# Masks and adjacency earlier in the first group, and the next norm tied behind the attention's last product

## The chip, the cores and the metric

The kernel runs on one core of a Trainium2 chip. The metric is device time in microseconds (us) of one execution; the median of four runs before the change is 2364.11 us (2363.8 to 2365.03). Engine names are those of the profile: PE is TensorE (PEld its weight load), DVE is VectorE, ACT is ScalarE, POOL is GpSimd, SP is SyncE, which here only issues transfers. Each engine works through its own list of instructions strictly in order; an instruction that waits holds up everything behind it on that engine.

## The reference

A graph attention layer with a norm ahead of it, over 128 graphs of 64 nodes with 512 features, all float32. One adjacency matrix (64 x 64) serves all graphs. Cut to what matters here:

```
h = relu(layernorm(x))                                   # x: [128, 64, 512]
def gat(x, W, a):                                        # W: [H, F, O]
    Wh = einsum('bnf,hfo->bhno', x, W)
    f1, f2 = Wh . a[:, :O], Wh . a[:, O:]
    e = leaky(f1[..., :, None] + f2[..., None, :], 0.01)
    e = where(adj > 0, e, -1e9)
    return einsum('bhnm,bhmo->bhno', softmax(e), Wh)
h   = elu(gat(h, W_heads, a_heads))                      # 4 heads, joined to [b, n, 2048]
out = elu(gat(h, W_out, a_out))                          # 1 head
y   = relu(out @ w1 + b1) @ w2 + b2 + out
x + layernorm(y) * gamma + beta
```

## The kernel before, in words

Two graphs make a tile of 128 rows, so there are 64 tiles; four tiles make a group, and there are 16 groups. The large products (`project1`, `project2`, the two of `feed_forward`) use a seven-product scheme for 2 x 2 blocks (Strassen-Winograd), so sums of blocks are formed ahead of the products on POOL and DVE (`z_sums`, `sums`, the subtractions of `project2`'s `post`).

**A group's way.** `norm1(t)` takes a tile of x through `norm_stats` (L340-350): `bn_stats` (L343), `bn_aggr` (L345) and an add (L347) on DVE, a power (L349) on POOL; then a product on POOL (L357, tile `n1nb`) and the relu with scale and bias on ACT (L359), which writes `hn`. For the last two tiles of a group POOL adds two halves (L362, `hns`). `transpose_h` (L368-373) turns `hn` on PE (`pth`) and copies it to `hT` on ACT. `project_f` makes the scores' terms, `scores1` and `softmax` the attention weights, `transpose_weights` turns them. `attend1` (L510-539) multiplies the weights with `hn` on PE (L525, tiles `pz`, `pzS`); of each pair of result banks ACT copies one (L535) and DVE the other (L537) into `z`. `project1` makes the heads from z, `project2` (L604-628) the second layer's projection; `stage_e` is the second attention and `feed_forward` the rest.

**Who runs beside whom.** The main loop is over groups g. While `project2(g)` runs on PE, `attend1(g + 1)` and the norms, transposes, scores and softmax of group g + 2 are put between its products by `run` (L251-258). So beside `project2(0)` lie `attend1(1)` (tiles 4 to 7) and the norms of tiles 8 to 11.

**What sets the order.** The code's order is not the order on the engines. A scheduler sorts each engine's instructions by dependencies and priorities when the kernel is built, and an instruction may be placed far ahead of where the code has it. Tiles come from pools: `x` has four buffers (L94), `hn` four (L358), so the norm's relu of tile 8 waits until the attention's products of tile 4 have read `hn`, and the load of tile 12 (L95, from `prefetch`) waits until that relu has read x of tile 8. The results of `pth` use a pool of two PSUM buffers (`aux`, L81), those of `pz` and of the projections a pool of six banks (`bank`, L78).

**The queues.** SP issues the loads of x (L95), of the small first inputs (L100, L104, L107) and of all weight pieces (L238), in order. ACT's queue issues the four loads of W_heads (L150) at the start, POOL's the other weights and the stores of their sums (L222).

**The first group.** Before the main loop stand the loads, `norm1` of tiles 0 to 3, `masks()` (L117-135: `wa`, `blkones`, the sums over the identity `id32`, `headrow`, `isf`, `par`, `isq`, the adjacency mask `negm` from `aj`, and `eye`), and `fold_dve` (L173-181: 24 products with a sum on DVE, tile `jk`), which reads the PSUM banks that `spread_a` filled (`pab`, L158). `fold_pe` (L183-197: `pwt`, `wT`, `pwa`) needs banks that `fold_dve` frees.

In code, what the change touches is the order of the first loads and of two calls, and the first instruction of the norm:

```python
    for m in range(H):
        fetch(m)
    for t in range(G):
        norm1(t)
    masks()
    ...
        nc.vector.bn_stats(st, src)
```

Of the kernel before, what the change touches and what calls it, by code (L numbers as in the profile page):

```python
# [22 lines left out]
def gat_preln_kernel(  # L23
# [28 lines left out]
    nc = tc.nc  # L52
    P = 128
    B, N, F = x.shape
# [4 lines left out]
    NB = P // N  # L59
# [32 lines left out]
    def load(t, name="x"):  # L92

        tl = wk.tile([P, F], FP, tag="x", name=f"{name}{t}", bufs=4)  # L94
        nc.sync.dma_start(out=tl, in_=xf[ts(t, P), :])  # L95
        return tl

    X[0] = load(0)
    ar = wk.tile([2 * H, O], FP, tag="elu", name="ar", bufs=3)
    nc.sync.dma_start(out=ar, in_=a_heads.rearrange("h (r p) -> (h r) p", p=O))  # L100
    for t in range(1, G):
        X[t] = load(t)
    ah = wk.tile([2 * H * KC, P], FP, tag="elu", name="ah", bufs=3)
    nc.sync.dma_start(out=ah, in_=a_heads.rearrange("h (r p) -> (h r) p", p=P))  # L104
    aj = const.tile([P, N], mybir.dt.int32, name="aj")
    for b in range(NB):
        nc.sync.dma_start(out=aj[ts(b, N), :], in_=adj)  # L107

    negm = const.tile([P, N], FP, name="negm")
    blkones = const.tile([P, NB, N], FP, name="blkones")  # L110
# [6 lines left out]
    def masks():  # L117

        nc.vector.memset(wa, 0.0)
        id32 = const.tile([P, 32], FP, name="id32")  # L120
        nc.vector.tensor_reduce(id32, ident.rearrange("p (j r) -> p r j", r=32), AX.X, ALU.add)
        nc.vector.tensor_add(headrow, id32[:, 0:H], id32[:, H:2 * H])
        nc.vector.tensor_reduce(isf, id32[:, 0:2 * H].rearrange("p (c h) -> p c h", c=2), AX.X, ALU.add)
        for q in range(2):
            par = sm.tile([P, 1], FP, tag="par", name=f"par{q}")
            nc.vector.tensor_reduce(
                par, ident.rearrange("p (a q r) -> p q a r", a=2, q=2)[:, q], AX.XY, ALU.add
            )
            nc.vector.tensor_scalar(isq[:, q], isf, par, None, ALU.mult)
        nc.vector.memset(blkones, 0.0)  # L130
        for b in range(NB):
            nc.vector.memset(blkones[ts(b, N), b, :], 1.0)
        nc.vector.tensor_scalar(negm, aj, 0.0, None, ALU.is_gt)
        nc.vector.tensor_scalar(negm, negm, NEG, -NEG, ALU.mult, ALU.add)
        nc.vector.tensor_add(eye, ident[:, 0:N], ident[:, N:2 * N])
# [11 lines left out]
    def fetch(m):  # L147
        MT[m] = big.tile([P, KC, O], FP, tag=homes[m], name=f"pw{m}")
        queue = nc.scalar if m < H else nc.gpsimd
        queue.dma_start(out=MT[m], in_=mats[m].rearrange("(k p) o -> p k o", p=P))  # L150
# [88 lines left out]
        return w  # L239


    late = []

    def nothing():
        pass
# [5 lines left out]
    def run(steps, side=()):  # L251

        side, done = list(side), 0
        for i, fn in enumerate(steps):
            fn()
            while done * len(steps) < (i + 1) * len(side):
                side[done]()
                done += 1
# [81 lines left out]
    def norm_stats(src, tag, t):  # L340

        st = sm.tile([P, 6], FP, tag=tag + "st", name=f"{tag}st{t}")
        nc.vector.bn_stats(st, src)  # L343
        mv = sm.tile([P, 2], FP, tag=tag + "mv", name=f"{tag}mv{t}")
        nc.vector.bn_aggr(mv, st)  # L345
        ve = sm.tile([P, 1], FP, tag=tag + "ve", name=f"{tag}ve{t}")
        nc.vector.tensor_scalar(ve, mv[:, 1:2], EPS, None, ALU.add)  # L347
        rstd = sm.tile([P, 1], FP, tag=tag + "rs", name=f"{tag}rs{t}")
        nc.gpsimd.tensor_tensor(rstd, ve, mhalf, ALU.pow)  # L349
        return mv[:, 0:1], rstd  # L350
# [159 lines left out]
    def attend1(g):  # L510
        z = {}
        ZB[g] = z

        def task(j, half):
            t = G * g + j
            nm = ("11", "12")[half] if j < 2 else ("S1", "22")[half]
            if nm not in z:
                z[nm] = big.tile([P, H, 2, T], FP, tag="z" + nm, name=f"z{nm}_{g}")
            src, off = (HNS[t], 0) if nm == "S1" else (HN[t], half * T)
            at = AT[t]  # L520
            banks = [bank(f"pz{nm}_{t}_{b}") for b in range(NB)]
            for c in range(2):
                for b in range(NB):
                    rows = slice(b * N, (b + 1) * N)
                    nc.tensor.matmul(  # L525
                        banks[b][:, c, :].rearrange("p (h n) -> p h n", h=H),
                        src[rows, off + c * P:off + (c + 1) * P],
                        at[rows, b], start=True, stop=True, skip_group_check=True,
                    )
            for b in range(NB):  # L530
                n0 = (j % 2) * P + b * N
                dst = z[nm][:, :, :, n0:n0 + N].rearrange("p h c n -> p c h n")
                srcv = banks[b].rearrange("p c (h n) -> p c h n", h=H)
                if b == 0:
                    nc.scalar.copy(dst, srcv)  # L535
                else:
                    nc.vector.tensor_copy(dst, srcv)  # L537

        return [lambda j=j, half=half: task(j, half) for j in range(G) for half in range(2)]
# [64 lines left out]
    def project2(g):  # L604
        slot = {1: "11", 2: "12", 3: "12", 4: "22", 5: "S1", 6: "11", 7: "S1"}
        h1 = dict(H1)
        wh = big.tile([P, G, FO], FP, tag="wh2", name=f"wh2_{g}")
        WH2[g] = wh

        def post(what, a, b=None, to=None):  # L610
            behind = {"s1": ("11", "S1", "11"), "s5": ("S1", "22", "11"), "c11": ("12", "12", "11")}
            if what in behind:
                dst, x0, x1 = (h1[n] for n in behind[what])
                for h in range(H):
                    nc.gpsimd.tensor_tensor(dst[:, h], x0[:, h], x1[:, h], ALU.subtract)  # L615
            if what[0] != "c":
                return
            r, c = quadrant(what)
            dst = wh[:, 2 * r:2 * r + 2, c * Q:(c + 1) * Q]
            if b is None:  # L620
                nc.scalar.copy(dst, a)  # L621
            else:
                nc.vector.tensor_tensor(dst, a, b, ALU.add)

        ms = [H + h for h in range(H)]
        return unit(
            f"b{g}", product_n(ms, lambda p, i: h1[slot[p]][:, i]), post, (1, 5, 6, 2, 7, 3, 4)
        )
# [136 lines left out]

    for m in range(H):
        fetch(m)
    for t in range(G):
        norm1(t)
    masks()  # L770
    ab = {m: spread_a(m) for m in (0, 1)}
    aT = turn_a()
    for t in range(G):
# [43 lines left out]
    for g in range(NG):  # L817
        if g >= 1:
            side = stage_e(g - 1)
        else:  # L820
            side = sum(stage_a(1), [])
            for i, m in ((5, 4), (9, 5), (12, 6), (17, 7)):
                side.insert(i, lambda m=m: more_sums(m))
        done, n = 0, 6 * H
        for i in range(n):
            if i % 6 == 0:
                steps = head0 if (g, i) == (0, 0) else project1(g, i // 6)
            if (g, i // 2) != (0, 0):
                steps[i % 6]()
            while done * n < (i + 1) * len(side):  # L830
                side[done]()
                done += 1
        flush_late()
        attn = attend1(g + 1) if g + 1 < NG else []
        norms, scores, turns = stage_a(g + 2)
        tr, ff, fin = feed_forward(g - 1) if g >= 1 else ([], [], [])
        if g == NG - 1:
            run(project2(g), tr + [nothing] * 6 + ff[:2])
            run(ff[2:], [
                lambda: [scores2(g, j) for j in range(G)], lambda: spread2(g), nothing, nothing,  # L840
                lambda: softmax2(g), *[nothing] * 7, lambda: transpose_weights2(g), nothing,
                *[lambda j=j: attend2(g, j) for j in range(G)], nothing,
            ])
            continue
        early = [lambda: z_sums(g + 1, 0)]
        first = mix(attn, tr)
        if g >= 1:
            first[5:5] = norms[:1]
            first[10:10] = norms[1:]
        if g == 0:  # L850
            def sums_late(m):
                fetch(m)
                weight_sums(m, LAST["A"])

            run(project2(g), first + early + norms + scores + turns + [
                load_rows, lambda: sums_late(M1), lambda: sums_late(M2)
            ])
        else:
            run(project2(g), first + mix(
                ff[:7] + early + ff[7:12] + fin[:1] + ff[12:13] + fin[1:2] + ff[13:],  # L860
                scores + [nothing] * 8,
            ) + mix(fin[2:], [nothing] + turns + [nothing] * 2))
# [32 lines left out]
```

## Time and profile before

| what | us |
|---|---|
| median of four runs | 2364.11 |
| the profiled execution's own time | 2363.88 |
| its span (first to last instruction) | 2362.1 |
| around the span | 1.8 |
| PE busy | 2319.2 (98%) |
| DVE, ACT, POOL busy | 1264.5, 911.9, 1026.7 |
| PE busy in 0 to 25, 25 to 50, 50 to 118 | 13.73, 17.17, 65.47 |
| PE busy in 118 to 150, 150 to 175 | 26.59, 23.23 |
| PE busy in 175 to 700 | 525.00 |

The last three rows come from the busy time by stretch. From 175 us on PE is busy without a break in the stretches looked at; what PE stands idle lies before that. A line of the timeline reads: start, duration, engine, line, operation, output and input tile, shape, count, and in brackets the idle time before it and what ended that. SPq, ACTq and POOLq lines are transfers being issued. A chain can be followed through the brackets: an instruction's releaser is the one whose end it waited for.

### The profile page before, as it was taken

The numbers are of one execution on the slowest core, as the hardware profiler recorded it, in microseconds if no ns is written. First come the engines' busy times: TensorE is split into PE (matmuls) and PEld (weight loads), VectorE is DVE, ScalarE is ACT, GpSimd is POOL, SyncE is SP. The second block draws the span as 40 slices with busy tenths as digits, with TensorE's granted clock in tenths as the row PEclk, the third lists the DMA queues.
The fourth block names the chain that finished last, engine by engine and source line by source line (L and its number), as shares of the span: only waits on it lengthen the run. The fifth ranks groups of instructions, "written<-read, shape, count | busy, mean of one in ns | idle before, by whom it ended". The sixth has DMA issues, their size and how long they took to land.

```text
span 2362.1 us, 32849 instructions
## 1 busy us (share of the span) xinstructions
PE 2319.2 (98%) x11805; PEld 1933.9 (82%) x11805; DVE 1264.5 (54%) x2210; ACT 911.9 (39%) x1623; POOL 1026.7 (43%) x917
## 2 busy tenths in 40 slices
PE   6989999999999999999999999999999999999997
PEld 4868787888878888787887878888788887878885
DVE  6625474554646556474554745556464563644527
ACT  2524425253352533425244252533525344251513
POOL 5663444425344353443524444253443534433333
PEclk9999999999999999999999999999999999999999
DMA  8545353444535445353453534445354453534443
GB/s 304 185 140 193 128 179 129 161 156 130 182 126 172 140 134 178 128 180 130 150 167 126 183 130 160 154 131 180 128 176 133 138 178 127 182 117 164 158 148 106
DMA packets 257809, 366.89 MB, mean 155 GB/s; under 512 B 22216, under 2 KB 145128, under 8 KB 257648
## 3 DMA queue, kind: packets, MB, share of 16 engines
q1 hardware_dynamic: 251024, 343.82, 43.5%
q0 software_dynamic: 4512, 16.78, 1.9%
q10 hardware_dynamic: 2112, 4.19, 0.5%
q8 instruction: 95, 1.56, 0.3%
q14 instruction: 66, 0.54, 0.1%
HBM read 337.45 MB, written 27.26 MB: 154 GB/s over the span
## 4 chain that ended last, share of the span: by engine, by line
PE 94%; DVE 2%; ACT 1%; POOL 1%; issue 1%; DMA 0%; DVEq 0%
PE g_b L322 33%; PE g_a L307 32%; PE g_c L307 8%; PE g_d L322 8%; PE pz L525 4%; PE pa L673 2%; PE pto L700 1%; PE pzS L525 1%; PE pth L371 1%; PE s1pt L472 1%; PE pf L381 1%; PE s1pe L406 1%; DMA x<-in_x_dram 0%; PE s2pt L667 0%; PE pwa L193 0%
## 5 line engine op out<-in xcount | busy, mean ns | idle before, releaser
L322 PE MATMUL g_b<-w,h 128*128 128x256 f32 x2560 | 598.0, 380 | 0.0
L322 PEld LDWEIGHTS g_b<-w,h 128*128 128x128 f32 x2560 | 479.9, 190 | 72.7 <-issue 10.1
L307 PE MATMUL g_a<-z,w 128*128 128x256 f32 x1520 | 360.9, 380 | 1.6 <-DVE g_a L581 0.7
L307 PE MATMUL g_a<-zs_z,w 128*128 128x256 f32 x1504 | 347.8, 379 | 0.0
L307 PEld LDWEIGHTS g_a<-z,w 128*128 128x128 f32 x1520 | 287.2, 190 | 58.6 <-issue 14.3
L307 PEld LDWEIGHTS g_a<-zs_z,w 128*128 128x128 f32 x1504 | 284.5, 190 | 50.8 <-issue 14.3
L322 PE MATMUL g_b<-w,hS 128*128 128x256 f32 x1024 | 243.7, 382 | 0.0
L585 POOL TENSOR_TENSOR hS<-hS,h 128x512 f32<-128x512 f32 x64 | 83.1, 1299 | 366.4 <-DVE hS L549 366.4
L547 ACT ACTIVATE exc<-g_a 128x512 f32<-128x512 f32 x256 | 152.4, 595 | 199.6 <-DVE g_a L581 119.3
L322 PEld LDWEIGHTS g_b<-w,hS 128*128 128x128 f32 x1024 | 191.4, 191 | 31.2 <-issue 6.7
L549 DVE SCALAR_TENSOR_TENSOR h<-exc,g_a 128x512 f32<-128x512 f32 x192 | 131.5, 685 | 137.9 <-ACT exc L548 136.7
L548 ACT ACTIVATE exc<-exc 128x512 f32<-128x512 f32 x256 | 161.6, 631 | 6.6
L615 POOL TENSOR_TENSOR h<-h,h 128x512 f32<-128x512 f32 x64 | 86.7, 1363 | 138.1 <-PE g_b L322 138.0
L332 POOL TENSOR_TENSOR zs_z<-zS,z 128x512 f32<-128x512 f32 x63 | 89.3, 1418 | 127.9 <-PE g_a L307 123.3
L615 POOL TENSOR_TENSOR h<-hS,h 128x512 f32<-128x512 f32 x64 | 81.3, 1271 | 142.3 <-PE g_b L322 142.3
L474 ACT COPY at<-s1pt 128x512 f32<-128x512 f32 x64 | 34.7, 588 | 279.8 <-PE s1pt L472 279.8
L307 PE MATMUL g_c<-ot,w 128*128 128x256 f32 x512 | 123.9, 385 | 0.8 <-DVE ot L710 0.8
L322 PE MATMUL g_d<-w,rt 128*128 128x256 f32 x512 | 121.4, 380 | 1.7 <-DVE o L740 1.0
L307 PE MATMUL g_a<-zS,w 128*128 128x256 f32 x496 | 117.2, 379 | 0.0
L639 DVE SCALAR_TENSOR_TENSOR jf<-wh,ao 128x512 f32<-128x512 f32 x128 | 92.9, 763 | 40.9 <-ACT wh L621 40.7
L333 POOL TENSOR_TENSOR zs_z<-z,zs_z 128x512 f32<-128x512 f32 x63 | 85.8, 1363 | 61.5 <-PE g_a L307 41.1
L307 PEld LDWEIGHTS g_c<-ot,w 128*128 128x128 f32 x512 | 93.8, 190 | 21.9 <-issue 9.3
(159 smaller groups left out, 3537.7 us busy)
## 6 DMA issues: line engine op xcount, KB each, us to landing
w<-tc SPq DMA_DIRECT2D x632, 256.0 KB, 2.6
w<-in_L_gnn_W_heads_dram SPq DMA_DIRECT2D x192, 256.0 KB, 2.8
w<-in_L_gnn_W_out_dram SPq DMA_DIRECT2D x192, 256.0 KB, 2.7
w<-in_L_gnn_w_dram SPq DMA_DIRECT2D x96, 256.0 KB, 2.7
x<-in_x_dram SPq DMA_DIRECT2D x66, 256.0 KB, 3.7
xr<-in_x_dram SPq DMA_DIRECT2D x64, 256.0 KB, 2.7
out_dram<-o SPq DMA_DIRECT2D x64, 256.0 KB, 2.1
tc<-pt POOLq DMA_DIRECT2D x20, 512.0 KB, 5.7
```

The source lines that it names most:

```text
L307: nc.tensor.matmul(bk[:, o, :], w[:, k, ts(o, P)], a[:, k, :], start=start and o == 0 and k == 0, stop=k == 1, skip_group_check=True,)
L322: nc.tensor.matmul(bk[:, j, :], a[:, k, ts(j, P)], w[:, k, :], start=start and k == 0 and j == 0, stop=i == len(ms) - 1 and k == 1, skip_g ...
L332: eng.tensor_tensor(s2, s1, a11, ALU.subtract)
L333: eng.tensor_tensor(s4, a12, s2, ALU.subtract)
L525: nc.tensor.matmul(banks[b][:, c, :].rearrange("p (h n) -> p h n", h=H), src[rows, off + c * P:off + (c + 1) * P], at[rows, b], start=True ...
L547: nc.scalar.activation(ex, src, AF.Relu, scale=-1.0)
L548: nc.scalar.activation(ex, ex, AF.Exp, scale=-1.0)
L549: nc.vector.scalar_tensor_tensor(dst, ex, -1.0, src, ALU.add, ALU.max)
L585: nc.gpsimd.tensor_tensor(dst, dst, H1["22"][:, h], ALU.add)
L615: nc.gpsimd.tensor_tensor(dst[:, h], x0[:, h], x1[:, h], ALU.subtract)
L639: nc.vector.scalar_tensor_tensor(junk, WH2[g][:, j], 1.0, ao[:, c, :], ALU.mult, ALU.mult, accum_out=f[:, c, j:j + 1],)
L673: nc.tensor.matmul(pa, AT2[g][:, j, :], WH2[g][:, j, :], start=True, stop=True)
```

## The change

Three things are changed. The adjacency load (two transfers, one for each half of the partitions) moves from the end of the first loads to directly behind the first tile of x. The call of `masks()` moves ahead of the four `norm1` of the first group. And the norms that lie beside `project2(0)` (tiles 8 to 11) get an added dependency: their first instruction, `bn_stats`, waits for the last product of the attention put down so far, which is the last product of `attend1(1)`.

```diff
     X[0] = load(0)
+    aj = const.tile([P, N], mybir.dt.int32, name="aj")
+    for b in range(NB):
+        nc.sync.dma_start(out=aj[ts(b, N), :], in_=adj)
     ar = wk.tile([2 * H, O], FP, tag="elu", name="ar", bufs=3)
...
     nc.sync.dma_start(out=ah, in_=a_heads.rearrange("h (r p) -> (h r) p", p=P))
-    aj = const.tile([P, N], mybir.dt.int32, name="aj")
-    for b in range(NB):
-        nc.sync.dma_start(out=aj[ts(b, N), :], in_=adj)
...
-    late = []
+    late, GATE = [], {}
...
-        nc.vector.bn_stats(st, src)
+        first = nc.vector.bn_stats(st, src)
+        if "pe" in GATE:
+            tc.add_manual_dep(
+                first.ins, GATE["pe"].ins.name,
+                mybir.DependencyInfo(mybir.DependencyClass.Sync, mybir.DependencyReason.DATA),
+                reason="x comes late: in VectorE's order behind the attention",
+            )
...
-                    nc.tensor.matmul(
+                    LAST["pz"] = nc.tensor.matmul(
...
+    masks()
     for t in range(G):
         norm1(t)
-    masks()
...
+            def gated(fn):
+                GATE["pe"] = LAST["pz"]
+                fn()
+                GATE.clear()
+
+            norms = [lambda fn=fn: gated(fn) for fn in norms]
             run(project2(g), first + early + norms + scores + turns + [
```

How the two built programs differ in the order on each engine (no time is in this):

- PE: the same order.
- DVE, first group: the adjacency mask (L133, L134) stands behind the norm of tile 0 instead of behind that of tile 3; `par`, `isq`, `isq`, `eye` stand together ahead of the `bn_aggr` and add of tiles 2 and 3, and these four small instructions are now the last ahead of `fold_dve`.
- DVE, later: the `bn_stats` of tiles 8 to 11, with their `bn_aggr` and add, leave their places among the first `attend1` and `project1`, and those of tiles 12 to 15 leave their places among the copies of `attend1(1)` (L537). All eight now stand behind its last copy, in the order of the tiles; the add of `project2` (L272, `g_b`), which stood behind the norm of tile 15, stands behind the `bn_stats` of tile 13.
- POOL: the powers and products (L349, L357) of tiles 8 to 11 stand behind the last of the six sums of `z_sums` (L332, L333, L334), one pair after the other.
- ACT: the relus of tiles 8 to 11 stand together behind the last copy of `attend1(1)`, and ahead of the copies `hT` and `t_b`.
- SP: the adjacency loads are second and third; the loads of x for tiles 12 to 15 stand behind the pieces `w_7` instead of among `w_2` and `w_7`, two of them among `w_3`.

## The prediction

> **What bounds the kernel now.** I read the page first, then who PE waited for, then the timeline where it waited. The page says that PE is busy 98% of the span, and of the 40 slices (59 us each) only the first, the third and the last are not full of PE:
>
> ```profile
> PE 2319.2 (98%) x11805; PEld 1933.9 (82%) x11805; DVE 1264.5 (54%) x2210; ACT 911.9 (39%) x1623; POOL 1026.7 (43%) x917
> ...
> PE   6989999999999999999999999999999999999997
> ```
>
> So a gain can come only from PE's idle time in the first three slices (to about 165 us; behind that the stretches show none), and whatever is gained there moves everything after it by as much: behind it the order on every engine is the same in both programs. PE's waits between 45 and 170 us, as total, times and longest:
>
> ```profile
> PE pzS L525 <- DVE z L537: 5.4, 1, 5.4
> PE s1pt L472 <- DVE s1A L435: 5.4, 1, 5.4
> PE pth L371 <- ACT hT L373: 1.8, 1, 1.8
> ...
> PE g_a L307 <- ACT at L474: 0.6, 1, 0.6
> ```
>
> The second is the first softmax at 48 us, which the change leaves alone. The first is what the gate is about. The timeline there:
>
> ```profile
> 136.41 0.69 DVE L343 BATCH_NORM_STATS2 n1st<-x 128x6 f32<-128x512 f32 x1 [11.77 <-DMA x<-in_x_dram]
> 137.02 0.67 DVE L537 COPY z<-pz 128x512 f32<-128x512 f32 x1
> ...
> 137.75 1.35 PEld L525 LDWEIGHTS pzS<-at,hns 64*128 64x128 f32 x6 [5.81 <-DVE z L537]
> ...
> 147.85 0.70 DVE L343 BATCH_NORM_STATS2 n1st<-x 128x6 f32<-128x512 f32 x1 [3.32 <-DMA x<-in_x_dram]
> ...
> 159.81 0.70 DVE L272 TENSOR_TENSOR g_b<-g_b,s_b 128x512 f32<-128x512 f32 x1
> ...
> 161.66 0.66 PE L371 MATMUL pth<-ident,hn 128*128 128x128 f32 x4 [1.77 <-ACT hT L373]
> ```
>
> DVE stands 11.77 us before a bn_stats (tile 12) whose x is in flight; behind it are the copies that free the banks of `pz`, and PE stops for 5.41 us. A second cost comes with it, seen in two stretches of the busy time table (PE busy second, granted clock after POOL's column):
>
> ```profile
> 139.00:140.00 1.00, 1.00 (x3) 0.35 (x3) 0.42 (x2) 0.59 (x1) 0.00 (x0) 0.50 0.00 0
> ...
> 160.00:162.00 2.00, 0.34 (x3) 0.34 (x4) 0.51 (x1) 1.46 (x3) 0.81 (x1) 1.00 0.42 131
> ```
>
> The clock is 0.50 from 134.9 to 141.7 us; eight products take 2.96 us instead of 1.99.
>
> **The change, part by part.** The profiled execution took 2363.88 us (span 2362.1, 1.8 around it), 0.23 below the median 2364.11.
>
> *Gate: what goes.* PE passes 131.64 us as before. After that stand four `pz` blocks, three blocks of `g_b` between them and no late copy: a block `pz` and one `g_b` took 2.98 us three times from 122.68 on, 1.06 of it `pz`. So 3 x 2.98 + 1.06 = 10.0: the attention ends at 141.6 instead of 149.7 (148.61 + 1.14). That is 8.1 us: 5.4 waited, the rest slow clock.
>
> *Gate: what is late next.* The norms of tiles 8 to 11 now wait too, and on POOL they stand behind the six sums. Forward from 141.6: the copy of the last `zS` on DVE follows PE's 138.66 and ends at 139.4. POOL then does L332, L332, L333, a subtraction (L615), L333, L334, L334: 7 x 1.24 (two L332 took 2.50 from 149.28) = 8.7, to 148.1. Power and product of one tile take 0.93 (158.55 to 159.48): tile 8 ready 149.0, tile 9 at 150.0; the relu on ACT takes 0.81. PE, through `g_b` of the third product since 148.65 (four blocks, 7.0), waits for `hn` 8 (149.9) and 9 (150.85) with its `pth`, then does 1.9 of `g_b` to 153.2. Tiles 10 and 11: `bn_aggr` needs POOL's product of 8 and 9, the add follows at 150.4, POOL's pairs end at 151.3 and 152.3, the relus at 152.2 and 153.1; only then does ACT copy `hT` of tile 8 (to 153.65), which frees the buffer for `pth` of tile 10.
>
> Meanwhile SP can load x of tile 13 only when `hn` 9 is made. From the start of a relu to the start of the bn_stats that reads the load it released were 3.51 us (144.34 to 147.85 for tiles 10 and 14) and 3.63 (150.26 to 153.89), so bn_stats 13 starts at 153.5 and L272 behind it at 154.1. From L272 to the next `g_b` before: 159.81 to 162.32 (161.66 + 0.66), 2.51, through `t_b`, `hT` 9, `pth` 11, the same order as now. So this `g_b` starts at 156.6 instead of 162.3: **-5.7 us** remain of 8.1. Bounds: all 8.1 if nothing waits; -2.8 if x of tile 13 lands in 5.54 like tile 12's (130.85 to 136.39) instead of 2.65. I take -5.7, because SP has nothing else to issue just before these loads, as at 145.18.
>
> The waits behind the SP loads are hidden: `w_3` stands behind x of tile 13 (issued about 150.9) and is first used at 176.68 - 5.7 = 171. The gate itself adds nothing to PE, which waits for none of the gated stats before `pth`. U (L389), behind the stats of 14 and 15 (about 157.7), waits for its product until 162 anyway.
>
> *The clock again.* PE's new waits are 1.25, 0.35, 0.5 and 1.75 us with work between. Over 3.41 us stretches (half of the 6.83 us for which the clock was 0.50) PE would be busy 34 to 60%. It fell after a stretch busy 25% (131.5 to 134.9) and did not after one busy 48% (158.8 to 162.2). So 0 is nearest; at worst half speed for 6.8 us, +3.4.
>
> [...]
>
> *Stats of tiles 8 and 9 leave 57 us.* Ahead of a copy DVE waited 1.97 us for x (57.54, bn_stats) and the copy ran 58.15 to 58.82; PE's next product started 58.92, although it could after 58.30 (its own end, and ACT's copy of the bank at 58.27). The chain to 66.00 (exc, h, three copies, L332) hangs on it: **-0.55**; bounds 0 (if `at`, which the profile names, releases it) and -0.6. I take -0.55, since `at` (58.75) ends no later than the copy and feeds a later product.
>
> *Masks and adjacency.* Here 24 folds on DVE set PE: `pwt` waits for the first folds, then `pab`, `pth`, `pwa` without a gap.
>
> ```profile
> 12.68 1.30 DVE L122 TENSOR_TENSOR headrow<-id 128x4 f32<-128x4 f32 x1
> ...
> 15.38 1.08 DVE L134 TENSOR_SCALAR negm<-negm 128x64 f32<-128x64 f32 x1
> 16.38 1.33 DVE L135 TENSOR_TENSOR eye<-ident 128x64 f32<-128x64 f32 x1
> ```
>
> With the `isq` at 14.13 (1.08) four tiny operations take over 1 us: each ends when the 1.26 us sum running on POOL ends. Now `negm` is done while POOL is idle (before 10.5; the adjacency is ahead of x of tile 1 in the same queue, so nothing waits for it alone), but the second `isq`, free before, gets its place in that row. The adjacency ahead of x delays tiles 1 and 2 by at most what both loads took behind `ah` (0.65; 0 if they fit into 2.99 to 5.6 us, where SP's queue moved only `ar`), and with them POOL's row; I take 0.4. If `headrow` gets in before POOL's next sum, three operations are held, and the folds start at 16.40 + 0.4 + 0.5 (four small operations that now come last) = 17.3 instead of 17.77: -0.45. If not, four are held: 17.62 + 0.9 = 18.5, +0.75. x of tile 3 must now wait for W_heads' first load (6.45), so it decides. I take the middle, **+0.15**.
>
> [...]
>
> **Sum.** -5.7 - 0.55 + 0.15 = -6.1: 2363.88 - 6.1 = 2357.8, as a median 2358.0 (-0.26%).
>
> **The rivals.** (1) *The wait moves to x of tile 13* (landing 5.5): L272 is 2.9 later, 2360.9. For: tile 12's load; against: the two after it. (2) *The clock falls in the new waits*: up to +3.4, 2361.4. For: 34% is near 25%. (3) *Less is late*: if the norms slip between POOL's sums or nothing waits behind them, -8.1 - 0.55 - 0.45: 2355.0. Against: POOL's order. (4) *Slower*: x of tile 13 lands very late. Each us costs one once L272 hangs on it; at 2.65 + 6.1 = 8.8 us the gain is gone, with a clock loss of 2.2 as before already at 6.6; slower by 0.2% needs 11 to 13. Loads of x took up to 10.2 in the first 70 us, but with the queues full. At 11.3 with the clock loss: 2369. (5) *The change does nothing*: if the scheduler's order held DVE elsewhere, 2364; against: the DVE order shows all copies ahead of the stats.
>
> **How the numbers follow.** 0.2% is 4.7 us, about what a measurement can tell from no change. Chances: forecast (2356 to 2359.4) 0.61; (1) 0.12; (2) 0.12; (3) 0.07; (4) 0.05; (5) 0.03. Faster by 0.2%: forecast and (3), 0.68. Same: (1), (2), (5), 0.27. Slower 0.05. The range 2356.2 to 2361.8 leaves out (3), (4), (5) and little else; the forecast's own is 2356 to 2359.4.
>
> **What would show it.** Right: no wait of `pzS` on a DVE copy and clock 1.00 there; the last `pz` about 8 us earlier; `pth` waiting for `hn` twice, then for `hT`; L272 5 to 6 us earlier; `g_a` without the 0.6. Wrong: a stretch at 0.50 after 145, a bn_stats that waits over 4 us for x with L272 behind it, `fold_dve` starting after 18.5, or a new long DVE operation beside POOL (one `s1A` took 5.17 at 104.39) on PE's path.

## The result and the profile after

The changed kernel takes 2360.93 us (median of 35 runs, 2358.42 to 2363.37) beside 2364.17 us for the kernel before (55 runs, 2361.87 to 2366.66): a ratio of 0.9985, 95% interval 0.998 to 0.9989. That is 0.15% faster, inside the range of the prediction (2356.2 to 2361.8) and a little over half of the 0.26% forecast. It is outside the forecast's own range (2356 to 2359.4), at the prices of its rivals (1) and (2). The profiled execution took 2360.1 us (span 2358.3) beside 2363.88 (span 2362.1), so it shows 3.8 of the 6.1 us that the sum had.

The first lines of the page of the changed kernel, and of its 40 slices that of PE. PE's busy time fell by 2.7 us, and its third slice, in which the stop at 132 to 138 us lay, went from 8 to 9 tenths:

```profile
PE 2316.5 (98%) x11805; PEld 1932.1 (82%) x11805; DVE 1263.6 (54%) x2210; ACT 911.8 (39%) x1623; POOL 1028.0 (44%) x917
...
PE   6999999999999999999999999999999999999997
```

What PE waited for between 45 and 170 us in the changed kernel (total, times, longest):

```profile
PE s1pt L478 <- DVE s1A L441: 5.4, 1, 5.4
PE pth L377 <- ACT hT L379: 2.2, 2, 1.9
PE pth L377 <- ACT hn L365: 1.4, 2, 1.2
PE g_a L307 <- DVE zs_z L332: 0.9, 1, 0.9
PE g_a L307 <- DVE g_a L587: 0.7, 1, 0.7
```

The wait of `pzS` on the copy `z`, 5.4 us, is gone, and so is that of `g_a` on `at`. The waits of `pth` are the ones that the prediction put in their place. The timeline of the changed kernel from the sums to the last product of the third block, to be read as a chain from top to bottom:

```profile
139.75 2.49 POOL L332 TENSOR_TENSOR zs_z<-zS,z 128x512 f32<-128x512 f32 x2 [0.56 <-DVE zS L543]
...
141.76 7.17 PE L322 MATMUL g_b<-w,h 128*128 128x256 f32 x32
...
149.28 1.69 ACT L365 ACTIVATE hn<-x,n1nb,n1rs 128x512 f32<-128x512 f32 x2 [6.84 <-POOL n1nb L363]
...
150.15 0.66 PE L377 MATMUL pth<-ident,hn 128*128 128x128 f32 x4 [1.22 <-ACT hn L365]
...
153.80 0.69 DVE L343 BATCH_NORM_STATS2 n1st<-x 128x6 f32<-128x512 f32 x1 [0.16 <-DMA x<-in_x_dram]
...
154.41 0.68 DVE L272 TENSOR_TENSOR g_b<-g_b,s_b 128x512 f32<-128x512 f32 x1
...
156.25 1.12 PE L377 MATMUL pth<-ident,hn 128*128 128x128 f32 x4 [1.91 <-ACT hT L379]
```

The attention's last product is done before 141.76, where the kernel before had 149.68. POOL's sums, the first relu at 149.28, the bn_stats of tile 13 at 153.80 and L272 at 154.41 stand within 0.3 us of where the prediction put them (149.1, 153.5, 154.1). Then comes a thing that it had not counted: four `pth` take 1.12 us instead of 0.66, and sixteen products of `g_b` behind them 4.85 instead of 3.62. The busy time by stretch of the changed kernel says why (stretch, length, PE, PEld, DVE, ACT, POOL busy, granted clock, DMA share, GB/s):

```profile
152.82:156.23 3.41, 1.24 (x7) 0.60 (x5) 2.30 (x7) 1.92 (x5) 1.91 (x5) 1.00 0.89 279
156.23:159.64 3.41, 3.40 (x10) 2.93 (x11) 1.73 (x4) 1.04 (x2) 1.90 (x3) 0.50 0.66 225
```

The new waits leave PE busy for 1.24 of 3.41 us (36%), and for the next 3.41 us the clock is 0.50. This is one of the signs that the prediction had named for being wrong (a stretch at 0.50 after 145 us).

Where the time went, from starts of the same instruction in both traces: the first `g_a` 55.68 before and 56.15 after (+0.47, the first group); the `g_a` behind L332 66.00 and 65.88 (so -0.59 between the two); the last `g_a` of the third block 117.76 and 117.85 (+0.21); the products of `pf` behind the attention 165.71 and 161.93 (-3.87). Together -3.78, the whole difference of the spans (3.8). Behind `pf` the traces of the kernels here need 2196.4 to 2197.1 us to the end, so a difference of under 0.8 us between two spans need not come from a change.

### The profile page after: what moved, and what is told of

The parts are those of the page before. It is cut to its first block, busy times and chain, and to the rows that moved or that the text cites. A ratio compares the mean times of both kernels' runs of the same rounds, so it can differ in the third digit from the quotient of the medians.

```text
span 2358.3 us, 32855 instructions
## 1 busy us (share of the span) xinstructions
PE 2316.5 (98%) x11805; PEld 1932.1 (82%) x11805; DVE 1263.6 (54%) x2210; ACT 911.8 (39%) x1623; POOL 1028.0 (44%) x917
## 4 chain that ended last, share of the span: by engine, by line
PE 94%; DVE 2%; POOL 1%; ACT 1%; issue 1%; DMA 0%; SPq 0%; DVEq 0%; POOLq 0%
PE g_b L322 33%; PE g_a L307 32%; PE g_c L307 8%; PE g_d L322 8%; PE pz L531 4%; PE pa L679 2%; PE pto L706 1%; PE pzS L531 1%; PE pth L377 1%; PE s1pt L478 1%; PE pf L387 1%; PE s1pe L412 1%; DMA x<-in_x_dram 0%; PE s2pt L673 0%; PE pwa L193 0%
## 5 line engine op out<-in xcount | busy, mean ns | idle before, releaser
L332 POOL TENSOR_TENSOR zs_z<-zS,z 128x512 f32<-128x512 f32 x63 | 89.5, 1421 | 127.3 <-PE g_a L307 123.5
L333 POOL TENSOR_TENSOR zs_z<-z,zs_z 128x512 f32<-128x512 f32 x63 | 85.3, 1354 | 61.6 <-PE g_a L307 41.3
```

The costliest lines, as they stand in the source:

```text
L332: eng.tensor_tensor(s2, s1, a11, ALU.subtract)
L333: eng.tensor_tensor(s4, a12, s2, ALU.subtract)
```

## The experiments

Each kernel ran beside the kernel before on the same chip; ratios are against those runs. Differences of under 1 us are not resolved by the medians. They are read from the traces, of which each kernel has one.

**The gate alone.** The adjacency load and the call of `masks()` are put back.

```diff
     X[0] = load(0)
-    aj = const.tile([P, N], mybir.dt.int32, name="aj")
-    for b in range(NB):
-        nc.sync.dma_start(out=aj[ts(b, N), :], in_=adj)
...
-    masks()
     for t in range(G):
         norm1(t)
+    masks()
```

> The gate alone, with the first group's loads and masks as before. Theory (the gate is worth about 4 us after its own waits and one stretch at half clock, the first group costs 0.5): 2359.9, about 0.5 under the changed kernel's 2360.9, with a stretch at 0.50 near 153 to 160 us. Rival (the missing part was lost in the first group): the gate alone gives the whole 6 us, 2358.2, and no stretch at 0.50 after 55 us.

Measured: 2361.3 us (11 runs, 2357.62 to 2367.16), ratio 0.9982 (0.9972 to 0.9993). So the gate carries the gain. Its runs spread over 9.5 us, two of them (2365.75 and 2367.16) within what the kernel before took beside it (2363.95 to 2371.1); of these two no trace was kept. Its profiled execution (2362.38) shows both of the dangers of the prediction at once. From its timeline and its stretches:

```profile
154.47 0.69 DVE L344 BATCH_NORM_STATS2 n1st<-x 128x6 f32<-128x512 f32 x1 [1.30 <-DMA x<-in_x_dram]
155.08 0.68 DVE L273 TENSOR_TENSOR g_b<-g_b,s_b 128x512 f32<-128x512 f32 x1
...
157.83 5.73 PE L323 MATMUL g_b<-w,h 128*128 128x256 f32 x16
```

```profile
151.84:155.26 3.42, 1.52 (x8) 0.83 (x7) 1.67 (x4) 1.08 (x2) 1.28 (x2) 1.00 0.85 239
155.26:158.67 3.41, 1.75 (x6) 1.58 (x7) 2.24 (x8) 2.15 (x4) 2.57 (x5) 0.50 0.83 296
158.67:162.09 3.42, 3.42 (x9) 2.70 (x8) 0.62 (x3) 0.00 (x0) 0.80 (x2) 0.50 0.00 0
```

x of tile 13 lands later, L273 (the changed kernel's L272) starts at 155.08 although everything ahead of it ran 0.7 earlier than in the changed kernel, and the clock is 0.50 for two stretches instead of one. From the last `g_a` (117.13) to `pf` (163.49) this execution needed 46.36 us, only 1.59 less than before.

**The first group alone.** No gate.

```diff
     X[0] = load(0)
+    aj = const.tile([P, N], mybir.dt.int32, name="aj")
+    for b in range(NB):
+        nc.sync.dma_start(out=aj[ts(b, N), :], in_=adj)
...
+    masks()
     for t in range(G):
         norm1(t)
-    masks()
```

> The first group's part alone, without the gate. Theory: the folds start near 14.6 us but PE's pwa starts 0.4 to 0.5 us later than before, because POOL's row is held by x of tile 2; 2364.6, and the wait of 5.4 us for the copy behind a late x is there as before. Rival (this part lost 2 us or more): 2366 to 2367. Rival (the earlier folds are worth something): below 2363.5.

Measured: 2364.86 us (11 runs), ratio 0.9996 (0.9987 to 1.0005): no difference that can be told, and the stop at 136 us with its half clock stays. In the trace the first `g_a` stands at 56.12, 0.44 later than before.

**The half clock.** The changed kernel, with eight more transposes of the identity on PE, which wait for nothing that the rest makes, between the `pth` of tiles 10 and 11. Their result isn't used.

```diff
+        if t == 10:
+            pd = bank("fill").rearrange("p a b -> p (a b)")
+            for k in range(8):
+                fill = nc.tensor.transpose(pd[:, ts(k % 4, P)], ident, ident)
```

> The changed kernel with eight extra transposes of the identity on PE (1.7 us of work that nobody reads) put into the wait ahead of tile 11's transposes. Theory (the clock falls because that window is only about 36% busy and costs 1.7 us): the clock stays at 1.00 behind 55 us and the time falls by 1.7 to 2359.2, although PE does more. Rival (the waits alone cost the time, the clock nothing): 2360.9 as before or up to 0.3 more.

Measured: 2359.47 us (9 runs), ratio 0.9974 (0.9964 to 0.9983), with 1.04 us of added work. PE's timeline of this kernel:

```profile
154.78 1.04 PE L381 MATMUL fill<-ident 128*128 128x128 f32 x8
157.31 0.66 PE L377 MATMUL pth<-ident,hn 128*128 128x128 f32 x4 [1.49 <-ACT hT L389]
157.80 3.62 PE L322 MATMUL g_b<-w,h 128*128 128x256 f32 x16
```

```profile
154.23:157.64 3.41, 1.86 (x15) 1.63 (x16) 1.81 (x7) 1.47 (x4) 1.59 (x4) 1.00 0.90 284
```

No stretch at 0.50 comes between 55.24 and 171.30 us, where the stretches read of this trace end; `pth` takes 0.66 and `g_b` 3.62 again, the 1.7 us that the changed kernel lost. From the last `g_a` (118.46) to `pf` (161.35) it is 42.89 us instead of 44.08. At that place the trace has neither the half clock nor its 1.7 us. The whole span (2358.2 us) is only 0.1 less than that of the changed kernel, since this execution was 0.6 later at the last `g_a` and took 0.5 longer behind `pf`; and between the medians the intervals of the ratios overlap slightly.

The same eight transposes put into the kernel with the gate alone:

> e1_gate_only with the eight extra transposes of the identity between the transposes of tiles 10 and 11, as in e3_fill. In the profile of e1_gate_only the clock was 0.50 from 155.26 to 162.09 and g_b's 16 products took 5.73 instead of 3.62. Theory A (half clock behind the stretch with little work is what was lost): no 0.50 there, g_b x16 in 3.5 to 3.7, and 1.5 to 2.5 less than e1_gate_only: 2361.3 - 2 = 2359.3. Theory B (x of tile 13 is what was lost): the extra work changes nothing or costs up to 0.5: 2361.3 to 2361.8. The extra work computes nothing that is used.

Measured: 2359.35 us (11 runs), ratio 0.9979 (0.997 to 0.9988), against 0.9982 without them. Again no half clock in the stretches from 50.50 to 169.97 us, and from the last `g_a` (115.99) to `pf` (159.28) 43.29 us instead of 46.36. In the trace this is theory A, narrowly: the window with the transposes held 1.54 us. The medians do not tell the two kernels apart.

**Another place for the gate.** Only the norms of tiles 12 to 15 wait for the last product of `attend1(1)`; those of tiles 8 to 11 stay where they were. The first group is that of before.

```diff
+        if g == 1:
+            def gated(fn):
+                GATE["pe"] = LAST["end1"]
+                fn()
+                GATE.clear()
+
+            norms = [lambda fn=fn: gated(fn) for fn in norms]
         if g >= 1:
             first[5:5] = norms[:1]
...
+            LAST["end1"] = LAST["pz"]
```

> The same gate on the norms of tiles 12 to 15 (those whose x comes late) instead of tiles 8 to 11; first group as before. Theory (most of the 8 us was given back because the gated norms are the ones that the next transposes wait for): no wait for hn, at most 1 us for hT, no stretch at 0.50 behind 55 us, project2's second product of the second head near 153.5 instead of 162.3: 2355.3. Rival (the attention's copies are bound by something else, or the late x comes back as a wait of L272): 2358 or more.

Measured: 2355.23 us (5 runs, 2353.95 to 2355.55), ratio 0.9956 (0.9944 to 0.9968), the whole -0.4%. The timeline of this kernel at the place of the chain above:

```profile
148.71 1.04 PE L378 MATMUL pth<-ident,hn 128*128 128x128 f32 x8
...
151.28 0.70 DVE L273 TENSOR_TENSOR g_b<-g_b,s_b 128x512 f32<-128x512 f32 x1
...
153.14 0.66 PE L378 MATMUL pth<-ident,hn 128*128 128x128 f32 x4 [1.22 <-ACT hT L380]
...
153.63 3.62 PE L323 MATMUL g_b<-w,h 128*128 128x256 f32 x16
```

Tiles 8 to 11 are normed long before, `pth` waits for no `hn`, and of waits there only 1.2 us are left, less than the 1.8 of before. From the last `g_a` (117.79) to `pf` (157.18) it is 39.39 us, 8.56 less than before: the 8.1 us of the prediction with nothing given back, and 0.6 less waiting of `pth`. No stretch at 0.50 comes between 53.08 and 169.13 us (the mean granted clock of this execution is 0.999), and the five runs spread over 1.6 us. The stop was made by tile 12 alone (the bn_stats at 136.41 in the profile of before); the gate on tiles 8 to 11 moved it only because the bn_stats stand on DVE in the order of the tiles.

With a second wait, tiles 8 to 11 behind the last product of `attend1(0)`:

> The norms of tiles 12 to 15 wait for the last product of attend1(1), as in e4_gate_next, and those of tiles 8 to 11 for the last product of attend1(0). What it asks: is the -0.55 us that I gave to the stats of tiles 8 and 9 leaving the z copy at 58 us real? Theory A (swallowed): the first g_a product behind the copy starts at 58.8 or earlier and L332 is done about 0.1 to 0.6 earlier at 66, but the g_a chain at 104 to 117, which hangs on one DVE operation s1A held beside POOL's sums, starts no earlier than in e4, so the time is that of e4 within 0.3: 2355.0 to 2355.5. Theory B (it carries on): 0.5 less than e4, 2354.7. Theory C: the gate only moves the stats ahead of z_sums' DVE part, which sets g_a at 66, and it is 0.5 to 1 later than e4: 2355.9.

Measured: 2355.54 us (5 runs), ratio 0.996 (0.9947 to 0.9972), the same as without it. In the traces the second `g_a` comes 2.64 us behind the first (55.56, 58.20) instead of 3.34 (55.74, 59.08), and the last one 0.84 earlier, of which 0.18 was there at the first. So the 0.6 us of the stats that leave 57 us are real in the trace (theory B), and too small for the medians.

**Only the adjacency load earlier.**

> Against before: only the adjacency load moves behind the first tile of x. No gate, masks called behind the norms. Theory A (the load order costs): bn_stats of tile 2 starts 1.3 to 1.5 later than 9.65, POOL's row and hn of tile 3 as much later, pwa 0.4 to 0.6 later, as in e2_first_only; 2364.2 + 0.45 = 2364.7. Theory B (it was the order of the masks that cost): hn of tile 3 as in before, pwa at 29.55, 2364.2.

Measured: 2365.41 us (11 runs), ratio 1.0003 (0.9995 to 1.0012), not told apart from before. In the trace it is theory A, and more than it: `pwa` comes 1.08 us later than before, not 0.4 to 0.6. What the first group does is read better over the traces. The folds (`fold_dve`), the end of `hn` of tile 3, and the first `pwa` in us; the first four rows have the first group of before:

| kernel | bn_stats of tile 2 | first fold | `hn` 3 done | `pwa` |
|---|---|---|---|---|
| before | 9.65 | 17.77 | 27.43 | 29.55 |
| gate alone | 9.53 | 17.64 | 27.33 | 29.43 |
| gate, with transposes | 9.26 | 17.38 | 27.07 | 28.27 |
| tiles 12 to 15 / two gates | 9.69 / 9.45 | 17.80 / 17.68 | 27.48 / 27.24 | 29.59 / 28.79 |
| changed kernel | 11.11 | 14.61 | 29.00 | 30.01 |
| first group alone | 11.09 | 14.59 | 28.97 | 29.99 |
| changed, with transposes | 11.80 | 15.29 | 29.68 | 30.69 |
| adjacency load alone | 11.81 | 18.51 | 29.62 | 30.63 |

Every trace with the early adjacency has the stats of tile 2 later by 1.4 to 2.5 us, `hn` of tile 3 by as much, and `pwa` later than every trace without it, with early folds or late. The cost begins at SP. Before, it issues x of tile 1 at 1.58 us; in the changed kernel the two adjacency transfers take it 1.17 us, and x of tile 1 is issued at 3.05 and read at 9.63 instead of 8.21. So in the traces the order of the loads costs 0.4 to 1.1 us at `pwa`, which the medians do not resolve; with x of tile 1 late, the order of the masks only makes folds early that no longer decide.

**Masks that are really first.** The operations that need only the identity are tied ahead of the first bn_stats, into time in which DVE waits for the first x (`EARLY` holds `headrow`, both `isq` and `eye`); the two operations on `aj` leave `masks()` and stand behind the bn_stats of tile 3; the adjacency load stays in its old place. No gate.

```diff
+    masks()
     for t in range(G):
         norm1(t)
-    masks()
+    head = nc.vector.tensor_scalar(negm, aj, 0.0, None, ALU.is_gt)
+    tc.add_manual_dep(head.ins, LAST["st"].ins.name, ...)
+    nc.vector.tensor_scalar(negm, negm, NEG, -NEG, ALU.mult, ALU.add)
...
-        nc.vector.bn_stats(st, src)
+        first = nc.vector.bn_stats(st, src)
+        LAST["st"] = first
+        while t == 0 and EARLY:
+            tc.add_manual_dep(first.ins, EARLY.pop().ins.name, ...)
```

> Against before: the operations that need only the identity (id32, headrow, par, isf, isq, eye) stand ahead of the first norm on DVE, where DVE was idle while the first x was loading, the adjacency load stays in its old place, and the mask made from it stands behind the norm of tile 3. No gate. Theory A (what delayed the first group in the changed kernel was x of tiles 1 and 2 behind the adjacency, and with them POOL's row; the operations held by POOL only set when the folds start): folds start at 12 to 13 instead of 17.77, bn_stats of tile 2 at 9.7 as in before, hn of tile 3 ends at 27.4 or earlier, pwa starts 1.0 to 1.5 earlier than 29.55; 2364.2 - 1.2 = 2363.0. Theory B (the first group hangs on something else, the loads of W_heads): pwa at 29.4 to 29.7, 2364.2. The wait of 5.4 us at 136 and the half clock stay in both.

Measured: 2369.68 us (11 runs), ratio 1.0018 (1.0009 to 1.0027): slower, though the folds start at 11.40 and `pwa` at 26.94, 2.6 earlier than before. PE's waits and DVE's timeline:

```profile
PE s1pt L480 <- DVE s1A L443: 14.4, 1, 14.4
```

```profile
42.48 0.70 DVE L344 BATCH_NORM_STATS2 n1st<-x 128x6 f32<-128x512 f32 x1 [4.25 <-DMA x<-in_x_dram]
48.78 0.69 DVE L344 BATCH_NORM_STATS2 n1st<-x 128x6 f32<-128x512 f32 x1 [5.60 <-DMA x<-in_x_dram]
49.39 0.67 DVE L428 TENSOR_TENSOR s1e<-s1pe,negm 128x512 f32<-128x512 f32 x1
```

The wait that the gate had removed at 136 us turns up at another place: the bn_stats of tiles 6 and 7 stand ahead of the first softmax on DVE. Before, their x had landed by 40.76, ahead of the softmax's input (42.93); now the input is ready 2.6 earlier and x later, and the softmax stands behind two transfers until 49.39. SP issued these loads later too, from 32.63 us on instead of 29.31; what held SP is not separated by any run here. Theory A was right that `pwa` comes earlier (it had 1.0 to 1.5 us) and wrong about the time.

With the two gates as well:

> e5_two_gates and e6_masks_first together. If the gains add: e5 less 1.2, about 2354.0. If the first group's gain is lost again in the DVE chain at 104 to 117 us: as e5, 2355.2. If the new times bring another DVE operation beside POOL's sums, up to 1 us above e5.

Measured: 2357.65 us (6 runs), ratio 0.9966 (0.9954 to 0.9978). None of the three: 2 us slower than the two gates alone, with `s1pt` waiting 12.5 us.

So a third wait was added, the bn_stats of tiles 6 and 7 behind the softmax, to this kernel (shown here) and to that without the gates:

```diff
+        at = LAST["end"] if t in (6, 7) else GATE.get("pe")
...
-    softmax_end = LAST["A"]
+    softmax_end = LAST["end"] = LAST["A"]
```

> e8_all with one more wait: the bn_stats of tiles 6 and 7, which stood ahead of the first softmax on DVE and held it for 3.28 and 4.68 us there while their x was in flight, wait for the end of that softmax. Theory A (the whole loss of e8_all against e5_two_gates is DVE standing before those two x): the softmax starts when s1pe is ready, at about 40.3, the first g_a at 52.5 to 54 instead of 60.27 (5.4 us from s1pe to s1pt as in before; up to 1.2 for the two bn_stats, which now stand among the z copies), and everything behind it as much earlier: 2355.5 - 2.6 + 0.6 = 2353.5, between 2352.5 and 2354.5. Theory B (the loads themselves are late and something else waits for hn of tiles 6 and 7, pth at about 70, or for weights): the first g_a is early, but a wait of over 1 us comes at 60 to 90: 2355 to 2357.

> e6_masks_first with that wait alone (tiles 6 and 7 behind the softmax), no other gate. Theory A: s1pt waits 5.4 us instead of 14.43, so 9 us of e6 are gone; the stop of 5.4 us at 136 and its half clock stay. 2369.7 - 9 + 0.6 = 2361.3, between 2360.5 and 2362.5, so 2 to 3 less than before. Theory B: as under e9_three_gates, 2363 to 2365.

Measured: with the gates 2354.95 us (5 runs), ratio 0.9959 (0.9946 to 0.9971); without them 2364.77 us (11 runs), ratio 0.9995 (0.9986 to 1.0004). `s1pt` waits 5.4 us in both, as theory A has it, and comes at 45.91 and 44.76 instead of 48.28. Both medians are outside the ranges of theory A. In the first, the two bn_stats then stood among the `z` copies, PE waited 1.6 us ahead of the first `g_a`, and of 2.4 us only 0.5 were left there (55.16). The second is 3.5 us over the number of theory A. Its timeline at the stop that the gate would have taken away:

```profile
135.94 0.69 DVE L344 BATCH_NORM_STATS2 n1st<-x 128x6 f32<-128x512 f32 x1 [12.29 <-DMA x<-in_x_dram]
...
137.28 2.07 PE L539 MATMUL pzS<-at,hns 64*128 64x256 f32 x6 [5.93 <-DVE z L551]
```

The last `g_a` came 0.99 earlier than before (116.77), but x of tile 12 landed only 0.47 earlier (135.94 instead of 136.41), and the clock stayed at 0.50 for 10.24 us instead of 6.83. `pf` came at 166.28, 0.57 later than before. A gain ahead of a wait on a transfer was spent in that wait.

Last, the bn_stats of tiles 6 and 7 behind the first half of `attend1(0)`, so that they follow its four `z` copies:

```diff
-    softmax_end = LAST["end"] = LAST["A"]
+    softmax_end = LAST["A"]
...
+    LAST["end"] = LAST["pz"]
     head0 = project1(0, 0)
```

> e9_three_gates with the bn_stats of tiles 6 and 7 tied behind the last product of the first half of attend1(0) instead of behind the softmax, so that on DVE they stand behind its four z copies. In e9's profile the softmax came 2.4 earlier than in before (s1pt 45.91 instead of 48.28), but the two bn_stats stood among the z copies and the first g_a, at 55.16, was only 0.5 earlier. Theory A (1.5 to 1.9 of the softmax's gain lay in those copies): pz takes 5.3 instead of 5.83, the first g_a starts within 0.4 of its end, at 53.2 to 53.8, and all behind it is as much earlier: 2355.0 - 1.7 = 2353.3. Theory B (hn of tiles 6 and 7 is then late, or the sums of zS and z are): a wait of 1 to 2 us at 60 to 75, 2355.0.

Measured: 2352.36 us (6 runs, 2352.1 to 2352.61), ratio 0.9944 (0.9932 to 0.9955): 0.56% faster than before, and the fastest of all kernels here; its slowest run is faster than the fastest of the changed kernel by 5.8 us. Its first `g_a` starts at 53.14, 2.0 us earlier than in the kernel with the wait behind the softmax (theory A had 53.2 to 53.8, and 2353.3 us), and of its waits between 45 and 170 us these are the largest:

```profile
PE s1pt L493 <- DVE s1A L456: 5.4, 1, 5.4
PE pth L392 <- ACT hT L394: 1.2, 1, 1.2
PE g_a L314 <- DVE zs_z L339: 0.9, 1, 0.9
```

The largest wait left is that for the softmax itself, 5.4 us in which PE stands idle. No run here puts other work there.

## Why the prediction came out as it did

- **What goes at the gate (8.1 us): right.** The attention ends where it said (141.76 for 141.6), without a slow clock. The kernel with the gate on tiles 12 to 15 shows 8.56 us, 0.6 of it from `pth`, when nothing is given back.
- **What is late next (2.4 us): right**, term by term: POOL's row, the relus, x of tile 13, L272 at 154.41 for 154.1. That 2.65 us landing was the likelier one, but not by as much as the chances had it: in the gate alone L273 came some 1.4 us later, which is half of the first rival's price. In the changed kernel's trace L272 is 0.3 us off, so that the median equals rival (1)'s 2360.9 is chance.
- **The clock (0, at worst +3.4): the step that failed.** It cost 1.7 us in the changed kernel (1.12 - 0.66 and 4.85 - 3.62) and 2.6 in the gate alone. The text had both bounds, 25% busy fell and 48% did not, and called 34 to 60% nearer to the second; the window that came held 36%. The second rival was the true one at half of its price. Forecast and second rival both hold in part, which is why the time lies between 2358.0 and 2361.4. The 34 to 60% were themselves about right. What was missing is that the stretches of 3.41 us lie differently against the work from trace to trace: the first edge of one behind the last `g_a` comes 0.84 us after it in the changed kernel (156.23 - 117.85 less eleven stretches), 0.59 in the gate alone, 1.63 and 2.78 in the two kernels with transposes. The stretch at 152.82, with 1.24 us, is among the thinnest that this trace has (153.30 to 156.71 holds 1.23); half a stretch earlier and later, 151.10 to 154.51 holds 2.96 us and 154.51 to 157.92 holds 1.68. From these windows it is the author's estimate that the fall in this execution was partly chance, and that the term should have held a part of that price instead of 0.
- **The stats of tiles 8 and 9 (-0.55): right**, in size (-0.59 to 66 us) and in setting `at` aside: in the changed kernel the second `g_a` starts at 58.78, while the copy `at` (58.63 to 59.22), which the profile of before had named, is still running. 0.2 of it is given back by 118 us, for which no run here shows the cause.
- **Masks and adjacency (+0.15, bounds -0.45 and +0.75): inside the bounds, with the wrong mechanism.** The first folds start at 14.61, not at 17.3 or 18.5: only `headrow` was held by a POOL sum (0.97 us, to 13.74; the sum, L210, ran from 12.46 to 13.72). `par`, the two `isq` (0.37 together) and `eye` (0.21) ran from 13.73 to 14.34, most of it while POOL did two small products (13.71 to 14.21). But the folds no longer set PE; `pth` waited 5.2 us for `hn`. The delay of tiles 1 and 2 behind the adjacency was 1.4 us, not 0.4 (SP issued x of tile 1 at 3.05 instead of 1.58), and POOL's row carried it to `hn` of tile 3; x of tile 3, which the prediction took to decide, was read only 0.67 later (11.78 for 11.11). The error was to add a delay of x to the start of the folds, and not to follow it down POOL's row to its own end. The held operation and the free ones, in the changed kernel:

```profile
12.77 0.97 DVE L122 TENSOR_TENSOR headrow<-id 128x4 f32<-128x4 f32 x1
...
13.71 0.50 POOL L363 TENSOR_SCALAR n1nb<-n1mv,n1rs 128x1 f32<-128x1 f32 x2
...
13.86 0.37 DVE L129 TENSOR_SCALAR isq<-isf,par 128x2 f32<-128x2 f32 x2
```

- **The sum.** -6.1, plus 1.7 of clock, 0.3 in the first group, 0.2 given back ahead of 118 us and 0.2 at L272 make -3.7, beside the -3.8 of the profiles. The medians moved by 3.2.
- **The chances.** They took 0.2% for about what a measurement can tell from no change; the interval here is 0.998 to 0.9989.
- Rivals (3) and (5) fall: what is late next is there, and the change does what it says. Rival (4) did not come in any run of the changed kernel (the slowest is 2363.37).

## What to carry to other kernels

An engine that works in order should meet an instruction that waits for a transfer only where nothing urgent stands behind it (here 11.77 us of DVE before one bn_stats became 5.4 us of PE); look for the one instruction that blocks, and move that one, not the whole group ahead of it: here, with the first group as before, the wait on tiles 12 to 15 gave 0.44%, and the wait on tiles 8 to 11, which holds those of 12 to 15 behind it, gave 0.18%. After every such gain, ask which transfers are now late for work that has come earlier, since 2.6 us gained at 30 us became 6.5 lost at the first `g_a`. Where one stop is replaced by several short ones, add up the busy time in windows of the length at which the clock changed (3.41 us here), at the thinnest position they can take, before calling the clock unchanged.

## What had not been expected of the hardware

The clock's records change on a grid of 3.41 us: in the kernel before 24 such windows lie between the first record (53.00 us) and the fall at 134.92, and two more to 141.74. Over all traces here, in windows that ran at 1.00 between 50 and 168 us, it fell to 0.50 after windows with PE busy for 0.48 to 1.59 us (14 to 47%), and stayed at 1.00 after the others, with 1.54 us and more (45%). Inside 44 to 47% both came: 1.52 and 1.59 us were followed by half clock, 1.54 and 1.55 were not. So in these traces the busy share tells the two apart outside 44 to 47%, and no run here shows what decides inside; the added transposes brought that window to 1.86 us in one kernel (54%), but only to 1.54 in the other. Executions of the changed kernel go the same way: their medians are 2362.11, 2360.93 and 2358.98 us at a mean granted clock of 0.991, 0.992 and 0.993. Single ones overlap (up to 2362.16 at 0.993), and which of their stretches ran at half clock is not on record.

In some traces the clock's records begin late. In that of the kernel before the first is at 53.00 us, and ahead of it the profile shows 1.00, though eight transposes at 48.28 take 1.94 us; in the changed kernel the same eight take 1.94 us under a recorded 0.50, and eight at a recorded 1.00 (148.71 in the kernel with the gate on tiles 12 to 15) take 1.04. Ahead of 50 us a fall is recorded in the changed kernel at 23.11, behind a window with 3.08 us of products; the shares above are those from 50 us on.

In the kernel before, `isq` took 1.08 us beside a POOL sum of 1.26, and ended at 15.21 as the sum did at 15.18; in the changed kernel two of them together took 0.37 while POOL did two products of 0.25 us. Others ended long before the sum beside them: in the kernel before, `isf` at 13.90 took 0.15 us, two `bn_aggr` at 13.97 took 0.23 and `par` at 15.25 took 0.20, each while a sum of 1.26 us ran. No run here shows what tells the two kinds apart.
